# Attention scores in three PSUM tiles by turns, and one softmax shift per unit fetched by way of DRAM

## The chip, the cores and the metric

The kernel runs on one core of a Trainium2 chip. The metric is device time in microseconds (us): the median of repeated runs. A profile comes from one further execution, with its own time and span.

## What is computed

The reference is one pre-norm layer, on x of shape (2, 2048, 512) in float32: attention with 16 query heads and 2 key groups of width 32 and rotary positions, then a projection with weights and inputs rounded to fp8 e4m3. Cut to what matters:

```python
# attention: h = layernorm(x), per batch of 2048 rows
q = (h @ wq + bq).reshape(b, s, 16, 32)
k = (h @ wk + bk).reshape(b, s, 2, 32)
v = (h @ wv + bv).reshape(b, s, 2, 32)
q, k = rotary(q) * 32**-0.5, rotary(k)
scores = einsum('bqhd,bkhd->bhqk', q, repeat(k, 8)) * 32**-0.5
out = einsum('bhqk,bkhd->bqhd', softmax(scores), repeat(v, 8))
x = x + out.reshape(b, s, 512) @ wo + bo
# second half: e4m3 with one scale for all rows, one for the weight
x = x + scaled_mm(e4m3(layernorm(x)), e4m3(weight).T).astype(bfloat16)
```

A softmax does not change when a constant is taken from all scores of a query, so a kernel is free to choose the constant (the shift) as long as the exponentials neither overflow nor vanish.

## The kernel before

The work has three stages. First keys, values and the first queries are projected for one batch. Then attention runs. Then the second half rounds, transposes and multiplies all rows.

**Units.** Attention is cut into 64 units. A unit is 256 queries of four heads (a quad). It goes through 16 chunks of 128 keys, in four rounds of four chunks. One chunk is a PSUM tile of 128 keys x 4 heads x 256 queries, 1024 columns, two banks. TensorE (PE) fills it with two products of 512 columns (`probabilities`, L1022); ScalarE (ACT) takes the exponential of the tile in one instruction (L1031); VectorE (DVE) adds the two exponentials of a pair (`add_pair`, L1005). GpSimd (POOL) issues one accumulating DMA a round that adds the first pair of the round to the second (`accumulate`, L1035), and DVE joins two rounds' results (`join`, L1038). So the sums over keys are mostly made outside PE; what is left of them is summed over partitions by products with ones (`sum_up`, L986). The products of exponentials with values (`columns`, L968, 16 products a round) run one round behind (`weigh(*behind)`).

**Scores by difference.** There are two score tiles, `E` and `O`, of two banks each, taken by turns over the chunks. A tile is not cleared between chunks: the key operand `dkS` holds the difference between a key and the key 256 positions (`BACK`) earlier, so that a product added onto the tile of two chunks ago gives the scores of this chunk. Keys and queries are split into a high and a low half and stacked on the 128 rows.

**The shift.** It goes into the tile at the start of a unit, by products: `first_scores` (L523) multiplies the queries of the next unit with the first 128 keys, queries on the partitions, in rounds 0 and 1 (four products and one DVE reduction L531 each). `split_maxima` (L504, L505) splits each query's maximum for each head into two parts, `gather_maxima` transposes them on PE (L543) and copies them out of PSUM (`mT`, L547), and `probabilities` starts the first two chunks of a unit with four products each against the selector `sel` (L1013). So each query and head has a shift of its own.

**PSUM.** Eight banks: two score tiles (four), `s0` for first scores and transposes, `s1` for everything that is projected meanwhile, and two `av` banks. An `av` bank holds a unit's values in its first half and its sums in the second; units alternate between the two.

**Order.** All engines work in program order; the order is written out by hand (`tc.manual_schedule`, L1058 to L1121). In each round: chunks 0 and 1; their addition; the value products of the round before; in some rounds a sum of the unit before and its copies out of PSUM (`keep_values` L1056, the first step of `finish_heads` L939); up to two waiting VectorE pieces (`fill(ON_DVE, 2)`); chunks 2 and 3; their addition; the accumulation; the first scores in rounds 0 and 1; one or two waiting PE pieces (projection of later queries and keys, output projection, all L295) and again up to two VectorE pieces. Queries of a later quad are fetched from DRAM in round 1 (`landing`, four DMAs on SP's queue, L349). In attention, ACT issues no DMAs.

**After attention** `transposed` and `multiplied` (L1166, L1176) go through 32 tiles of 128 rows. At the end the largest sum (`seen`) is compared with a bound of 1e18 (`MOST_BITS`); only above it a second, slow path under `tc.If` computes everything again with a shift from all keys. Worked out from the reference's inputs, the sums stay far below the bound with either kind of shift.

Of the kernel before, what the change touches and what calls it, by code (L numbers as in the profile page):

```python
# [16 lines left out]
P = 128  # L17
# [10 lines left out]
def preln_attn_fp8_ffn_kernel(  # L28
# [56 lines left out]
    BACK = HB  # L85
    AV_BANKS = 2
# [24 lines left out]
    def bank(name, dtype=F32):  # L111
# [5 lines left out]
        if name[:2] in ("pk", "pq"):  # L117
            pool, tag = (ps_av, "av") if name[1] == "k" else (ps_s, "s1")
            return pool.tile(shape, dtype, tag=tag, name=name, bufs=AV_BANKS if tag == "av" else 1)
        spread[0] += 1  # L120
        return ps_t.tile(shape, dtype, tag="EO"[spread[0] % 2], name=name)
# [63 lines left out]
    sel = const.tile([P, 4, P], F32R, tag="sel", name="sel")  # L185
    nc.gpsimd.memset(sel.bitcast(F32), 0.0)
    for j in range(4):
        nc.gpsimd.memset(sel[j * HD : j * HD + 2, j, :].bitcast(F32), -1.0)
    mrow = const.tile([P, HB], F32R, tag="mrow", name="mrow")
    nc.gpsimd.memset(mrow.bitcast(F32), 0.0)  # L190
# [20 lines left out]
    def quantized_scale(amax, scale, inv, name):  # L211
# [8 lines left out]
        nc.tensor.matmul(down[:, :1], sel[:1, 0, :].bitcast(F32), whole, start=True, stop=True)  # L220
        nc.vector.tensor_scalar(scale, down[:, :1], -1.0 / E4M3_MAX, 1e-12, ALU.mult, ALU.max)
# [275 lines left out]
    split = []  # L497
    largest = {}

    def split_maxima():  # L500

        if split:
            mview, mx = split.pop()
            nc.vector.tensor_copy(mview[:, :, :, 0], mx)  # L504
            nc.vector.tensor_tensor(  # L505
                mview[:, :, :, 1], mx, mview[:, :, :, 0].bitcast(F32), ALU.subtract
            )
# [4 lines left out]


    def first_scores(u, i):

        k, half = units[u]
        if i == 0:
            largest[u] = small.tile([P, HT, 4], F32, tag="mx", name=f"mx_{u}")
        mx = largest[u]
        s = ps_s.tile([P, 4, FIRST], F32, tag="s0", name=f"s_{u}_{i}")  # L520
        at = (half * HT + i) * P
        for j in range(4):
            nc.tensor.matmul(  # L523
                s[:, j, :],
                qst[k][:, j, at : at + P],
                stacked["dkS"][:, group(k), :FIRST],
                start=True,
                stop=True,
                skip_group_check=True,
            )  # L530
        nc.vector.tensor_reduce(mx[:, i, :], s, AX.X, ALU.max)  # L531
        if i == HT - 1:
            mview = mrow.rearrange("p (i j r) -> p i j r", i=HT, j=4)
            split.append((mview, largest.pop(u)))

    maxima = {}

    def gather_maxima(u):

        split_maxima()  # L540
        tp = ps_s.tile([P, TB], F32, tag="s0", name=f"mtp_{u}")
        for i in range(HT):
            nc.tensor.transpose(  # L543
                tp[:, i * P : (i + 1) * P], mrow[:, i * P : (i + 1) * P].bitcast(F32), ident
            )
        mT = wide.tile([P, HB], F32R, tag="mT", name=f"mT_{u}")
        nc.scalar.copy(mT, tp[:, :HB])  # L547
        maxima[u] = mT
# [153 lines left out]
    with tc.manual_schedule():  # L702
# [25 lines left out]
        for i in range(HT):  # L728
            first_scores(0, i)
        run(first(kv[3], MIDDLE))  # L730
        gather_maxima(0)
        run(kv[3])

# [74 lines left out]
    seen = const.tile([P, len(units)], F32, tag="seen", name="seen")  # L808
# [125 lines left out]
    def finish_heads(u, both, sums):  # L934
# [4 lines left out]
        nc.scalar.activation(total, sums, AF.Copy, accum_out=seen[:, u : u + 1])  # L939
# [3 lines left out]
        nc.scalar.activation(guess, guess, AF.Exp, scale=-1.0)  # L943
# [63 lines left out]

    def probabilities(u, T, kc):

        k, half = units[u]  # L1010
        if kc < 2:
            for j in range(4):
# [45 lines left out]
    with tc.manual_schedule():  # L1058
        behind = None
        before = None  # L1060
        for u, (k, half) in enumerate(units):
# [13 lines left out]
            for r in range(ROUNDS):  # L1075
# [25 lines left out]
                if r == 2:  # L1101
                    split_maxima()
# [368 lines left out]
```

## Time and profile before

| | us |
|---|---|
| median of 3 runs (lowest, highest) | 1733.91 (1731.88, 1735.4) |
| the profiled execution | 1724.88 |
| its span, first to last instruction | 1723.0 |
| PE / DVE / ACT / POOL busy | 1575.1 / 1248.8 / 1236.4 / 317.1 |
| exponentials L1031, 1024 of them | 992.6 busy, 1024 ns each |
| value products L968 | 495.1 busy |
| score products L1022 | 680.0 busy, 442 ns each |
| additions L1005, 511 of them | 624.7 busy, 1223 ns each |
| granted TensorE clock from 100 to 1600 us | 1.00 |

A row of a page or an answer names line, engine and operation, what is written and read with partitions and elements, the count, then busy time and mean of one, and after the second bar the idle time before it with what ended it. TensorE's products overlap: one of them takes longer from its start to its end than the next one waits to start, so a group's cost is the distance from its start to the next group's start, not the sum of its durations. PEld is the loading of weights, which runs beside products. An arrow like `T L1022 <- ACT p L1031` reads: the products of L1022 waited for the exponential of L1031.

### The profile page before, as it was taken

How to read it: one execution, taken by the hardware profiler on the slowest of the kernel's cores; microseconds unless marked ns; L12 is line 12 of the kernel's file. 1: busy time of each engine (PE TensorE's matmuls, PEld its weight loads, DVE VectorE, ACT ScalarE, POOL GpSimd, SP SyncE). 2: the span in 40 equal slices, each digit the busy share in tenths (PEclk: the TensorE clock that was granted, in tenths of full speed). 3: DMA queues.
4: the chain of work that ended last, by engine and by line, in shares of the span. 5: the costliest groups of instructions: out<-in, count | busy, mean ns of one | idle time of the engine just before them, and what ended most of it. 6: DMA issues, size and time to landing. Idle time of an engine off the chain costs nothing.

```text
span 1723.0 us, 33241 instructions
## 1 busy us (share of the span) xinstructions
PE 1575.1 (91%) x13483; PEld 900.6 (52%) x13483; DVE 1248.8 (72%) x1673; ACT 1236.4 (72%) x1629; POOL 317.1 (18%) x381
## 2 busy tenths in 40 slices
PE   5499999999999999999999999999999989999565
PEld 2255555555555555555555555555555555555222
DVE  4447677677887769776877687767777686676697
ACT  2257877777777777777777777877777777777375
POOL 3321112211212112211221122111211122111100
PEclk9699999999999999999999999999999999999888
DMA  6657769867778767878786688656867597576222
GB/s 203 201 122 178 170 146 216 195 127 160 184 178 164 183 153 160 192 147 195 175 196 134 118 199 177 152 117 154 184 149 154 105 203 145 116 187 138 56 86 112
DMA packets 105810, 272.61 MB, mean 158 GB/s; under 512 B 15920, under 2 KB 16560, under 8 KB 102960
## 3 DMA queue, kind: packets, MB, share of 16 engines
q0 software_dynamic: 41328, 142.10, 44.2%
q1 hardware_dynamic: 61904, 126.92, 25.3%
q8 instruction: 108, 1.77, 0.4%
q10 hardware_dynamic: 2416, 1.38, 0.3%
q14 instruction: 54, 0.44, 0.1%
HBM read 87.36 MB, written 40.89 MB: 74 GB/s over the span
## 4 chain that ended last, share of the span: by engine, by line
PE 67%; DVE 10%; DMA 8%; issue 7%; ACT 5%; SPq 2%; POOL 1%; ACTq 0%; DVEq 0%; POOLq 0%
PE avs L968 23%; PE T L1022 23%; PE po L295 5%; ACT p L1031 5%; PE pq L295 4%; PE T L1013 3%; PE avs L986 3%; PE s L523 2%; DMA pa<-pa 2%; DMA qst<-q_far 2%; PE pk L295 2%; PE mtp L543 1%; DVE v L236 1%; DVE pa L1005 1%; DMA sw_q<-q 1%
## 5 line engine op out<-in xcount | busy, mean ns | idle before, releaser
L1031 ACT ACTIVATE p<-T 128x1024 f32<-128x1024 f32 x1024 | 992.6, 1024 | 178.3 <-PE T L1022 171.1
L1005 DVE TENSOR_TENSOR pa<-p,p 128x1024 f32<-128x1024 f32 x511 | 624.7, 1223 | 356.1 <-ACT p L1031 355.0
L1022 PE MATMUL T<-qst,dkS 128*128 128x512 f32 x2048 | 680.0, 442 | 24.8 <-ACT p L1031 23.8
L968 PE MATMUL avs<-p,vX 128*32 128x256 f32 x8192 | 495.1, 382 | 0.0
L1022 PEld LDWEIGHTS T<-qst,dkS 128*128 128x128 f32 x2048 | 338.7, 188 | 273.6 <-ACT p L1031 153.5
L1035 POOL DMA_DIRECT2D pa<-pa x255 | 221.0, 867 | 1201.2 <-DVE pa L1005 915.3
L968 PEld LDWEIGHTS avs<-p,vX 128*32 128x32 f32 x8192 | 239.9, 109 | 225.8 <-issue 93.9
L1038 DVE TENSOR_TENSOR pa<-pa,pa 128x1024 f32<-128x1024 f32 x125 | 152.3, 1219 | 16.0 <-DMA pa<-pa 15.9
L295 PE MATMUL po<-wo_sb,attn 128*128 128x512 f32 x256 | 129.6, 603 | 0.0
L295 PE MATMUL pq<-xnT_q,wq_sb 128*128 128x512 f32 x224 | 111.8, 601 | 0.0
L1013 PE MATMUL T<-mT,sel 128*128 128x256 f32 x512 | 94.5, 307 | 6.5 <-ACT p L1031 6.1
L1013 PEld LDWEIGHTS T<-mT,sel 128*128 128x128 f32 x512 | 72.9, 188 | 46.9 <-ACT p L1031 30.8
L986 PE MATMUL avs<-pa,ones 128*32 128x256 f32 x1048 | 80.7, 382 | 11.9 <-DVE pa L1038 11.1
L531 DVE TENSOR_REDUCE mx<-s 128x4 f32<-128x512 f32 x128 | 87.5, 683 | 2.8 <-PE s L523 2.8
L1056 ACT COPY both<-avs 128x256 f32<-128x256 f32 x64 | 23.9, 373 | 86.7 <-PE avs L986 86.7
L523 PEld LDWEIGHTS s<-dkS,qst 128*128 128x128 f32 x512 | 77.2, 192 | 14.7 <-DVE mx L531 3.1
L939 ACT ACTIVATE both<-avs 128x256 f32<-128x256 f32 x64 | 24.6, 385 | 71.7 <-PE avs L986 71.7
L523 PE MATMUL s<-dkS,qst 128*128 128x128 f32 x512 | 72.8, 265 | 2.2 <-DVE mx L531 2.1
L295 PEld LDWEIGHTS po<-wo_sb,attn 128*128 128x128 f32 x256 | 44.3, 190 | 17.6 <-issue 11.0
L986 PEld LDWEIGHTS avs<-pa,ones 128*32 128x32 f32 x1048 | 27.8, 109 | 43.7 <-DVE pa L1038 30.4
L295 PEld LDWEIGHTS pq<-xnT_q,wq_sb 128*128 128x128 f32 x224 | 39.4, 190 | 17.4 <-issue 13.5
L1171 PE MATMUL xtp<-ident_bf,xq 128*128 128x128 bf16 x128 | 16.0, 266 | 34.3 <-DVE xq L237 34.3
(128 smaller groups left out, 1033.0 us busy)
## 6 DMA issues: line engine op xcount, KB each, us to landing
pa<-pa POOLq DMA_DIRECT2D x255, 512.0 KB, 5.2
qst<-q_far SPq DMA_DIRECT2D x128, 256.0 KB, 7.0
q_far<-hi_q SPq DMA_DIRECT2D x32, 256.0 KB, 4.6
q_far<-lo_q SPq DMA_DIRECT2D x32, 256.0 KB, 4.5
x_res<-in_L_attn_x_dram SPq DMA_DIRECT2D x16, 512.0 KB, 10.8
x_res<-in_L_attn_bo_dram POOLq DMA_DIRECT2D x32, 256.0 KB, 6.7
out_dram<-v SPq DMA_DIRECT2D x16, 512.0 KB, 2.8
sw_q<-q SPq DMA_DIRECT2D x240, 32.0 KB, 3.1
```

The costliest lines, as they stand in the source:

```text
L295: nc.tensor.matmul(dst, lhs(c), rhs(c), start=(c == 0), stop=(c == chunks - 1))
L523: nc.tensor.matmul(s[:, j, :], qst[k][:, j, at : at + P], stacked["dkS"][:, group(k), :FIRST], start=True, stop=True, skip_group_check=True,)
L531: nc.vector.tensor_reduce(mx[:, i, :], s, AX.X, ALU.max)
L939: nc.scalar.activation(total, sums, AF.Copy, accum_out=seen[:, u : u + 1])
L968: nc.tensor.matmul(av[j * HD : (j + 1) * HD, :], vX[batch(k)][:, kc, group(k), :], p[:, j, :], start=(kc == 0), stop=(kc == NTS - 1), tile ...
L986: nc.tensor.matmul(dst[j * HD : (j + 1) * HD, :], ones, part[:, j, :], start=start and i == 0, stop=stop and i == len(parts) - 1, tile_pos ...
L1005: nc.vector.tensor_tensor(pa, a, b, ALU.add)
L1013: nc.tensor.matmul(T[:, j, :], sel[:, j, :], maxima[u], start=(j % 2 == 0), stop=True, skip_group_check=True,)
L1022: nc.tensor.matmul(T[:, j : j + 2, :], stacked["dkS"][:, group(k), kc * P : (kc + 1) * P], qst[k][:, j : j + 2, half * HB : (half + 1) * H ...
L1031: nc.scalar.activation(p, T, AF.Exp, scale=SCALE)
L1035: nc.gpsimd.dma_start(out=to, in_=of, accum_op=ALU.add)
L1038: nc.vector.tensor_tensor(to, to, of, ALU.add)
```

## The change

Scores go through three tiles `T0`, `T1`, `T2` by turns, so the key difference reaches back 384 positions. The first scores of a unit take a turn of their own: after 16 chunks comes a 17th turn, in which the first 128 keys meet the queries of the unit after next, keys on the partitions as in any chunk. VectorE reduces this tile to one number a partition. ACT's queue then sends the 128 numbers to DRAM (round 1 of the next unit) and fetches all of them back onto every partition (round 2); VectorE takes their maximum, scales it, and all 16 exponentials of the unit get this one number as a bias operand. The shift products, their selector, the splitting, transposes and copy of maxima are gone. There is one `av` bank instead of two, a tile that all units share: values are copied out in round 0, and the sums of a unit are formed in rounds 1 and 2 of the next (in rounds 0 and 2 before). The join of round 1 stands ahead of chunks 2 and 3 and their addition, not behind. Fetched queries are asked for in round 0. The reciprocals of the sums are accumulated into `seen` beside the sums. After attention, transposes alternate between `s1` and `av`, and products go through three tiles.

```diff
-    BACK = HB
-    AV_BANKS = 2
+    RING = 3
+    BACK = RING * P
-    def first_scores(u, i):
+    def first_scores(u, tag):
...
-        s = ps_s.tile([P, 4, FIRST], F32, tag="s0", name=f"s_{u}_{i}")
-        at = (half * HT + i) * P
-        for j in range(4):
+        s = ps_t.tile([FIRST, 4, HB], F32, tag=tag, name=f"s_{u}")
+        for j in range(0, 4, 2):
             nc.tensor.matmul(
-                s[:, j, :],
-                qst[k][:, j, at : at + P],
+                s[:, j : j + 2, :],
                 stacked["dkS"][:, group(k), :FIRST],
+                qst[k][:, j : j + 2, half * HB : (half + 1) * HB],
                 start=True,
                 stop=True,
             )
-        nc.vector.tensor_reduce(mx[:, i, :], s, AX.X, ALU.max)
+        largest[u] = small.tile([P, 1], F32, tag="mx", name=f"mx_{u}")
+        nc.vector.tensor_reduce(largest[u], s.rearrange("p j t -> p (j t)"), AX.X, ALU.max)
+    def put_largest(u):
+        far = dram.tile([P, 1], F32, tag=f"largest_{u % 2}", name=f"largest_{u}")
+        nc.scalar.dma_start(far, largest.pop(u))
+        largest_far[u] = far
+    def fetch_largest(u):
+        every = wide.tile([P, P], F32, tag="every", name=f"every_{u}", bufs=2)
+        nc.scalar.dma_start(
+            every, largest_far.pop(u).rearrange("p e -> (p e)").partition_broadcast(P)
+        )
+        shift[u] = every
+    def make_shift(u):
+        every = shift[u]
+        shift[u] = small.tile([P, 1], F32, tag="shift_u", name=f"shift_{u}")
+        nc.vector.tensor_reduce(shift[u], every, AX.X, ALU.max)
+        nc.vector.tensor_scalar(shift[u], shift[u], -SCALE, None, ALU.mult)
...
-        nc.scalar.activation(guess, guess, AF.Exp, scale=-1.0)
+        nc.scalar.activation(guess, guess, AF.Exp, scale=-1.0, accum_out=seen[:, 1, u : u + 1])
...
+    def turn_of(u, i):
+        return f"T{(u * (NTS + 1) + i) % RING}"
-        if kc < 2:
-            for j in range(4):
-                nc.tensor.matmul(
-                    T[:, j, :],
-                    sel[:, j, :],
-                    maxima[u],
...
+        if kc < RING:
+            scores[kc] = ps_t.tile(
+                [P, 4, HB], F32, tag=turn_of(u, kc), name=f"T_{u}_{kc}"
+            )
+        T = scores[kc % RING]
...
-                start=False,
+                start=kc < RING,
...
-        nc.scalar.activation(p, T, AF.Exp, scale=SCALE)
+        nc.scalar.activation(p, T, AF.Exp, bias=shift[u], scale=SCALE)
...
+    avs = ps_av.tile([P, 2, HB], F32, tag="av", name="avs")
...
-                while r == 1 and landing:
+                while landing:
                     landing.pop()()
...
-                probs = [probabilities(u, banks[0], chunks[0])]
-                probs.append(probabilities(u, banks[1], chunks[1]))
+                probs = [probabilities(u, kc) for kc in chunks[:2]]
+                if r == 1 and 1 < u + 1 < len(units):
+                    put_largest(u + 1)
+                if r == 2 and 1 < u + 1 < len(units):
+                    fetch_largest(u + 1)
                 pair = add_pair(u, chunks[0], *probs)
                 if behind:
                     weigh(*behind)
                 if before and r == 0:
-                    parts = before.far[1 : 2 if in_two(before.u) else 3]
-                    sum_up(before.avs[:, 1, :], parts, False, False)
                     keep_values(before)
+                elif before and r == 1 and in_two(before.u):
+                    sum_up(avs[:, 1, :], before.far[1:2], False, False)
                 elif before and r == (2 if in_two(before.u) else 1):
-                    sum_up(before.avs[:, 1, :], before.far[3:], False, True)
...
+                    sum_up(avs[:, 1, :], before.far[3 if in_two(before.u) else 1 :], False, True)
+                    finishing.append(Job(finish_heads(before.u, before.both, avs[:, 1, :])))
                 fill(ON_DVE, 2)
-                if r == 2:
-                    split_maxima()
                 if last:
                     join(unit.far[1], unit.far[0])
+                elif before and r == 1 and in_two(before.u):
+                    join(before.far[3], before.far[2])
+                if last:
                     if u + 1 < len(units):
-                        gather_maxima(u + 1)
-
-                probs.append(probabilities(u, banks[0], chunks[2]))
-                probs.append(probabilities(u, banks[1], chunks[3]))
+                        make_shift(u + 1)
+
+                probs += [probabilities(u, kc) for kc in chunks[2:]]
                 if not (last and whole):
                     unit.far.append(add_pair(u, chunks[2], *probs[2:]))
                     accumulate(unit.far[r], pair)
                 add_some_bias()
-                if before and r == 1 and in_two(before.u):
-                    join(before.far[3], before.far[2])
                 behind = unit, chunks, probs
-                if r < HT and u + 1 < len(units):
-                    first_scores(u + 1, r)
+                if last and u + 2 < len(units):
+                    first_scores(u + 2, turn_of(u, NTS))
```

## The prediction

> **What bounds the kernel now.** The page's busy times come first, then the score line's own view, which says when attention begins and ends.
>
> ```profile
> PE 1575.1 (91%) x13483; PEld 900.6 (52%) x13483; DVE 1248.8 (72%) x1673; ACT 1236.4 (72%) x1629; POOL 317.1 (18%) x381
> ```
>
> ```profile
> L1031 ACT ACTIVATE p<-T x1024: 1003/1024/1062, 100.0 to 1605.3; 128x1024 f32<-128x1024 f32 x171
> ...
>   PE T L1022: 171.1, 316
> ...
>   PEld T L1022: 153.5, 372
>   PEld T L1013: 30.8, 62
> ```
>
> The exponentials run from 100.0 to 1605.3 + 1.0 us: 64 units in 1506.3 us, **23.5 us a unit**. Ahead lie 100 us, behind 116.7. PE looks full (91%), yet its products wait for ACT (the last two lines) and ACT's exponentials wait for PE (171.1): the two engines take turns. A unit's turns show in TensorE's timeline (start, length, then the group):
>
> ```profile
> 806.92 1.93 PE L968 MATMUL avs<-p,vX 128*32 128x256 f32 x32
> 808.79 0.44 PE L543 MATMUL mtp<-ident,mrow 128*128 128x128 f32 x2
> 808.98 1.18 PE L1022 MATMUL T<-qst,dkS 128*128 128x512 f32 x4
> 810.00 1.88 PE L295 MATMUL po<-wo_sb,attn 128*128 128x512 f32 x4
> 811.32 1.04 PE L1013 MATMUL T<-mT,sel 128*128 128x256 f32 x4
> 812.19 0.63 PE L1022 MATMUL T<-qst,dkS 128*128 128x512 f32 x2
> 812.66 0.64 PE L1013 MATMUL T<-mT,sel 128*128 128x256 f32 x4
> 813.14 0.63 PE L1022 MATMUL T<-qst,dkS 128*128 128x512 f32 x2
> 813.70 1.93 PE L968 MATMUL avs<-p,vX 128*32 128x256 f32 x32
> 815.45 0.61 PE L986 MATMUL avs<-pa,ones 128*32 128x256 f32 x8
> 815.99 1.20 PE L1022 MATMUL T<-qst,dkS 128*128 128x512 f32 x4
> 817.03 0.56 PE L523 MATMUL s<-dkS,qst 128*128 128x128 f32 x4
> 817.42 1.07 PE L295 MATMUL po<-wo_sb,attn 128*128 128x512 f32 x2
> ```
>
> Start to start is what a group costs when nothing is waited for. A chunk's two score products: 812.19 to 812.66, 0.47. A round's value products: 1.87 and 1.75, say 1.81. A sum: 0.54. One projection step: (1.88 - 0.59) / 3 = 0.43. So a unit's PE work is 16 x 0.47 = 7.5, plus 4 x 1.81 = 7.2, plus two sums 1.1, plus 480 projection steps over 64 units (7.5 x 0.43 = 3.2), plus the shift's products and the first scores 1.9 (next part), plus some 0.3 for the later keys: **21.2 us. The other 2.3 of the 23.5 are stalls.** The waits view allows this: products and loads wait 214 us for L1031 in all (153.5 + 30.8, and 29.9 on PE itself), 3.3 a unit, part of it under running products, and the sums wait 41.5 us for the joins (L1038).
>
> **The change, part by part (us per unit).**
>
> *Products removed.* The shift by product (L1013): 812.66 to 813.14, 0.48 a tile, two tiles: 0.96. Its transposes (L543): 0.19. The first scores (L523): 817.03 to 817.42, 0.39, twice: 0.78. Added: the 17th turn, two products like L1022: 0.47. PE net **-1.46**, 93 us over 64 units, all on the engine that is busiest. PE work becomes 19.8.
>
> *Three score tiles.* With two, chunk c+2 may not begin before the exponential of c ends: first product 0.24, its tail 0.40, exponential 1.02, and a wake of about 0.1: 1.75 from start to start. In a round's first half the value products cover that; in its second half PE has only 0.94 of scores and 0 to 0.9 of projection, and the second exponential ends 0.9 later still. Hence the 2.3 of stalls. With three, the chunk waits for an exponential one turn older (0.9 to 1.0 earlier), which covers nearly all of it. I leave 0.2 of score waits; bounds: 0, and the 2.3 of now.
>
> *Bias by pointer.* The exponentials take the shift as a per-partition bias. No row has an exponential with one; the nearest are a copy without and an ACTIVATE with, both 512 wide out of PSUM:
>
> ```profile
> L439 ACT ACTIVATE q<-pq,bq_sb 128x512 f32<-128x512 f32 x32 | 22.1, 689 | 3.7 <-PE pq L295 3.7
> ...
> L285 ACT COPY xnT_kv<-tp_kv 128x512 f32<-128x512 f32 x32 | 18.9, 590 | 20.8 <-PE tp_kv L282 20.8
> ```
>
> 0.10 each, so 1024 to about 1120 ns, and 16 x 0.10 = +1.6 on ACT. ACT's own sum: 16 exponentials 0.92 apart now (two in 1.94), 1.02 then: 16.3; keeping the values 0.37, the sums 0.39 + 0.19, Ln and Exp 0.84, a second accumulator read 0.19, query and key work 0.8; the mT copy (0.37) goes: 19.1. The two DMA issues: 0.5 to 0.7 each on ACT's queue in the prologue's rows, so between 0 (issued while an exponential runs) and 1.2; I take 0.3, since each stands behind an exponential of 1.1. ACT 19.4: just under PE. The added cost is hidden by PE only as long as PE is the slower; were ACT never hidden, 1.6 + 0.3 less 0.2 would be 1.7 a unit, 109 us.
>
> *The trip through DRAM.* The put stands behind exponential 5, the fetch behind 9, the shift's reduce in round 3, its use a round later. Behind the fetch on ACT wait the sums' copy and exponentials 10 and on; for them PE. The put has about a round, 5.2, to land. Rows for small transfers:
>
> ```profile
> sw_q<-q SPq DMA_DIRECT2D x240, 32.0 KB, 3.1
> ...
> bkv_sb<-in_L_attn_bk_dram ACTq DMA_DIRECT2D x1, 0.2 KB, 7.1
> ...
> bq_sb<-in_L_attn_bq_dram ACTq DMA_DIRECT2D x1, 2.0 KB, 11.1
> ```
>
> The last two ran at the start beside whole-block loads. I take the first, nearest in time and load: no wait. Bounds 0 and 11.1 - 5.2 = 5.9. The Trainium skill ("DMA: Bandwidth & Descriptors", "Anatomy of one DMA") puts the fixed cost of a DMA at about 2 us whatever its size; by it the sum has no wait at all, by the 11.1 row it has 5.9 a unit, and only the run can tell. The same page (Specifications) speaks against the put: runs under 512 B are read, modified and written, and this one writes 4-byte runs. Before unit 0 the trip costs a put and a fetch of 3 each around the key projection that fills 89.9 to 96.5 now: +0.5 in all.
>
> *VectorE.* Off: two reduces of 0.68 and two small operations of 0.17. On: one reduce of twice the width (about 1.28), one of 128 wide (under 0.3), one tiny multiply: even. DVE stays at 17.3 (1106 us busy from 100 to 1600, 63.8 units). But the new reduce stands behind the addition of chunks 14 and 15, and chunk 2 of the next unit needs its tile. After exponential 15 ends: addition 1.2, reduce 1.3, then PE may go on; PE gets there after two chunks' scores and the values, some 2.2 after the same moment, and round 3 on DVE (two additions, join, shift, reduce, fillers: over 6 us in a 5.2 us round) comes late. I price this **new stall at 0.7**, bounds 0 and 2 (a late filler piece of 1.2 more).
>
> *Joins and sums.* Two sums stay, one moved from round 0 to 1; the round 1 join stands ahead of an addition, so the sum of round 2 finds it done: of the 0.65 a unit of join waits 0.2 stays. In return the join comes about 5 us after its accumulation was issued, not 7.8 to 9.8 as now (six units from 350 to 480 us); landing takes 4.5 to 12.4, median 5.2. DVE will wait 0.5 to 1 there; its spare 3 us a unit hide it, else 1.0 x 64 = 64 us. One bank: values are copied out a round before the next values begin, so nothing waits. Query loads go to SP a round earlier and wait there for the old tile; what stands behind them on SP is needed later: 0. The epilogue's tiles: within 2 us.
>
> **The sum.** PE 19.8, stalls 0.2 + 0.7 + 0.2, and 0.2 for DMA slots and uneven units: **21.1 us a unit**, 1350 us. Span 1723.0 - 1506.3 + 1350 + 0.5 = 1567; with the 1.9 around it 1569. The profiled execution (1724.9) was 9 us quicker than the median of the runs (1733.9): 1578, say **1580**.
>
> **Rivals.**
> *Waits change place.* Only the products come off; the stall moves to ACT (longer exponentials) or the unit's border. 23.5 - 1.46 = 22.0 a unit: 1408, so 1637; with half of ACT's 1.7 showing, 1690. For it: ACT 19.4 against 19.8 is a tie, DVE with its DMA waits 18.5. Against: a third tile breaks just this turn-taking.
> *All stalls go.* 19.8 a unit: 1267, 1495. Against: the border stall.
> *The transfers hold the pace.* The windows view has the DMA engines 75% busy from 100 to 1600, 17.7 us a unit; at 21.1 that is 84%. If accumulations land so late that DVE stands, little is gained: 1690 to 1735.
> *Slower: the fetch blocks ACT.* If the put lands in 11.1, ACT has 19.4 + 5.9 = 25.3 a unit, 1.8 x 64 = 115 over now: 1850. It decides from a landing of about 5.2 + 4.1 = 9.3, where ACT reaches 23.5. Against: 32 KB moves in 3.1 under the same load.
>
> **Chances.** Forecast (1535 to 1610) 0.60; waits change place (1610 to 1690) 0.20; all stalls go (below 1535) 0.08; transfers 0.05, of which 0.03 within 0.2%; slower 0.07. Faster 0.90, same 0.03, slower 0.07 (0.2% is about what a measurement can tell from no change). Range: the forecast's own (0.60), the second up to 1670 (0.16) and the third down to 1525 (0.04): 1525 to 1670.
>
> **What would show it.** Right: PE's score products wait for L1031 under 60 us in all; exponentials near 1120 ns; a unit near 21; PE waiting for the first-score reduce about 0.7 a unit. Wrong: ACT idle behind its own DMA issue (put landing over 5), ACT busy without gaps at over 20 a unit, joins waiting for accumulations by more than 1.5 a unit, or score waits that stay.

## The result and the profile after

| | before | after |
|---|---|---|
| median of 4 runs (lowest, highest) | 1732.89 (1729.06, 1735.4) | 1866.03 (1854.8, 1875.69) |
| the profiled execution, its span | 1724.9, 1723.0 | 1865.6, 1863.8 |
| one unit, mean | 23.5 | 25.6 |
| granted TensorE clock, 300 to 1400 us | 1.00 | 0.93 |

The change makes the kernel slower: ratio 1.077, 95% interval 1.070 to 1.083. The forecast was 1580 with a range up to 1670. Busy times of the kernel after:

```profile
PE 1540.3 (83%) x12459; PEld 844.5 (45%) x12459; DVE 1249.2 (67%) x1609; ACT 1290.2 (69%) x1629; POOL 316.0 (17%) x376
```

Every engine now has more idle time than before. The exponentials' own view (minimum, median, maximum in ns; below, who waited for them):

```profile
L1025 ACT ACTIVATE p<-T,shift x1024: 1093/1114/1179, 106.7 to 1744.9; 128x1024 f32<-128x1024 f32 x171
...
  PEld T L1016: 129.6, 154
  PE T L1016: 64.9, 78
```

They have become as long as predicted (1114 ns at the median; 1115 on average). The new idle time lies elsewhere. From the DMA issues of the kernel after (KB each, median us from issue to landing):

```profile
largest<-mx ACTq DMA_DIRECT2D x64, 0.5 KB, 9.6
```

The prediction gave the put "about a round, 5.2, to land"; by this row it takes 9.6. The view tells the landing of only 11 of the 64 puts. A put adds 16 counts to its semaphore as it lands, and by these counts 59 puts can be timed: their median is 8.8, the shortest 7.0. ScalarE's timeline shows what that does to one unit:

```profile
789.77 0.33 ACTq L520 DMA_DIRECT2D largest<-mx  x1
790.47 1.12 ACT L1025 ACTIVATE p<-T,shift 128x1024 f32<-128x1024 f32 x1
792.72 4.13 ACT L1025 ACTIVATE p<-T,shift 128x1024 f32<-128x1024 f32 x4 [1.13 <-PE T L1016]
800.24 0.33 ACTq L526 DMA_DIRECT2D every<-largest  x1
801.74 0.39 ACT L930 ACTIVATE both<-avs 128x256 f32<-128x256 f32 x1 [4.89 <-PE avs L977]
```

The put goes out at 789.77. The last exponential ahead of the fetch ends at 796.85, but the fetch is not issued before 800.24: the put landed at 800.22. For 58 of the 59 puts that can be timed the fetch starts within 0.1 us of the landing. The chain of waits over the same stretch (start, length, what) shows that the put is not alone:

```profile
785.66 14.07 DMA pa<-pa
799.73 0.02 issue
799.76 1.24 DVE pa L1032
```

An accumulation issued 4 us ahead of the put took 14.07 us and landed within half a microsecond of it; the join waited for it, and the sum products for the join. The windows view of the stretch (length, busy us of PE, PEld, DVE, ACT and POOL with instruction counts, granted clock, DMA share, GB/s):

```profile
796.80:801.00 4.20, 0.00 (x0) 0.00 (x0) 1.24 (x2) 0.05 (x1) 0.00 (x0) 1.00 1.19 47
801.00:803.00 2.00, 1.97 (x12) 1.31 (x13) 2.00 (x2) 1.26 (x4) 0.59 (x2) 0.78 0.43 55
803.00:806.20 3.20, 3.20 (x6) 1.39 (x5) 2.07 (x3) 1.73 (x2) 1.17 (x2) 0.61 1.08 144
```

For 4.2 us TensorE does nothing, while the DMA engines count as fully busy and move 47 GB/s. They are busy with packets of other transfers that take longer than usual. The accumulations go in 32,640 packets of 4096 bytes, of which the median takes 0.33 us; here 764 of them take over 1 us, 730 of these while a put is on its way, against 8 in the kernel before. In this unit the put's own packets take 0.02 us at most. TensorE's timeline, to set beside the one of before:

```profile
794.80 1.93 PE L959 MATMUL avs<-p,vX 128*32 128x256 f32 x32
801.03 0.64 PE L977 MATMUL avs<-pa,ones 128*32 128x256 f32 x8 [4.30 <-DVE pa L1032]
801.60 1.67 PE L1016 MATMUL T<-qst,dkS 128*128 128x512 f32 x4
803.07 3.10 PE L291 MATMUL pq<-xnT_q,wq_sb 128*128 128x512 f32 x4
```

After the stop it goes on at a clock of 0.78 and 0.61: four projection steps take 3.10, where before the change four took 1.88. TensorE has 36 stops of over 2.5 us between 120 and 1600, where the kernel before has none; the granted clock averages 0.64 in the 5 us behind them and 1.00 in the 5 us ahead of them. In units 4 to 58 the mean time from exponential 9 to 10, where the fetch stands, went from 2.9 to 5.0 us.

### The profile page after: what moved, and what is told of

Same layout as the page of the kernel before. It is cut to its first block, busy times and chain, and to the rows that moved or that the text cites. A ratio compares the mean times of both kernels' runs of the same rounds, so it can differ in the third digit from the quotient of the medians.

```text
span 1863.8 us, 31217 instructions
## 1 busy us (share of the span) xinstructions
PE 1540.3 (83%) x12459; PEld 844.5 (45%) x12459; DVE 1249.2 (67%) x1609; ACT 1290.2 (69%) x1629; POOL 316.0 (17%) x376
## 4 chain that ended last, share of the span: by engine, by line
DMA 29%; PE 18%; DVE 17%; issue 16%; ACT 9%; SPq 5%; POOL 3%; ACTq 0%; DVEq 0%; POOLq 0%
DMA pa<-pa 10%; DMA largest<-mx 9%; PE T L1016 7%; ACT p L1025 7%; PE avs L959 5%; DMA sw_q<-q 4%; SPq L304 4%; DVE pa L996 4%; DVE pa L1032 2%; PE po L291 2%; POOL pa L1029 2%; DMA qst<-q_far 2%; PE pq L291 2%; DVE mx L515 1%; PE avs L977 1%
## 5 line engine op out<-in xcount | busy, mean ns | idle before, releaser
L1025 ACT ACTIVATE p<-T,shift 128x1024 f32<-128x1024 f32 x1024 | 1070.0, 1115 | 197.4 <-PE T L1016 137.3
L1016 PE MATMUL T<-qst,dkS 128*128 128x512 f32 x2048 | 726.0, 473 | 118.2 <-ACT p L1025 64.9
L1016 PEld LDWEIGHTS T<-qst,dkS 128*128 128x128 f32 x2048 | 375.3, 199 | 429.7 <-issue 176.4
L959 PE MATMUL avs<-p,vX 128*32 128x256 f32 x8192 | 511.2, 391 | 0.0
L930 ACT ACTIVATE both<-avs 128x256 f32<-128x256 f32 x63 | 24.2, 384 | 200.5 <-PE avs L977 99.9
L515 DVE TENSOR_REDUCE mx<-s 128x1 f32<-128x1024 f32 x64 | 77.9, 1218 | 2.6 <-PE s L507 2.6
L309 DVE SCALAR_TENSOR_TENSOR sw_q<-sw_q,sign,cs 128x512 f32<-128x512 f32 x30 | 22.5, 750 | 71.6 <-DMA sw_q<-q 49.8
L291 PEld LDWEIGHTS pq<-xnT_q,wq_sb 128*128 128x128 f32 x224 | 45.9, 205 | 23.5 <-issue 15.1
L507 PE MATMUL s<-qst,dkS 128*128 128x512 f32 x128 | 41.7, 409 | 5.5 <-DMA qst<-q_far 4.8
L278 PE MATMUL tp_kv<-ident,xn_kv 128*128 128x128 f32 x128 | 23.1, 325 | 27.4 <-DVE xn_kv L259 27.2
L291 PE MATMUL pk<-xnT_kv,wkv_sb 128*128 128x512 f32 x64 | 39.6, 738 | 7.3 <-ACT xnT_kv L281 7.3
L1177 PE MATMUL py<-wT,xqT 128*128 128x512 bf16 x128 | 43.1, 471 | 0.3 <-ACT xqT L1169 0.3
```

Source lines behind the costliest of these rows:

```text
L291: nc.tensor.matmul(dst, lhs(c), rhs(c), start=(c == 0), stop=(c == chunks - 1))
L507: nc.tensor.matmul(s[:, j : j + 2, :], stacked["dkS"][:, group(k), :FIRST], qst[k][:, j : j + 2, half * HB : (half + 1) * HB], start=True, ...
L515: nc.vector.tensor_reduce(largest[u], s.rearrange("p j t -> p (j t)"), AX.X, ALU.max)
L959: nc.tensor.matmul(av[j * HD : (j + 1) * HD, :], vX[batch(k)][:, kc, group(k), :], p[:, j, :], start=(kc == 0), stop=(kc == NTS - 1), tile ...
L1016: nc.tensor.matmul(T[:, j : j + 2, :], stacked["dkS"][:, group(k), kc * P : (kc + 1) * P], qst[k][:, j : j + 2, half * HB : (half + 1) * H ...
L1025: nc.scalar.activation(p, T, AF.Exp, bias=shift[u], scale=SCALE)
```

## The experiments

Ratios are to the kernel before, measured beside each run.

| run | us | ratio, 95% interval |
|---|---|---|
| e1_no_trip | 1680.9 | 0.971 (0.969 to 0.973) |
| e2_put_early | 1853.7 | 1.073 (1.070 to 1.075) |
| e3_trip_on_sp | 1816.4 | 1.050 (1.046 to 1.053) |
| e4_join_back | 1854.2 | 1.073 (1.071 to 1.075) |
| e7_put_act_fetch_sp | 1880.6 | 1.090 (1.086 to 1.095) |
| e8_rows_apart | 1684.6 | 0.976 (0.973 to 0.980) |
| e9_whole_rows | 1681.4 | 0.973 (0.969 to 0.977) |
| e11_scores_ahead_no_trip | 1673.4 | 0.969 (0.966 to 0.973) |
| e5_pointer_before | 1756.5 | 1.015 (1.012 to 1.018) |
| e6_two_tiles_no_trip | 1879.2 | 1.087 (1.084 to 1.090) |
| e12_repair | 1705.0 | 0.986 (0.983 to 0.989) |
| e13_repair_old_join | 1742.2 | 1.009 (1.006 to 1.012) |
| e15_rows_scores_ahead | 1679.4 | 0.971 (0.968 to 0.973) |
| e16_no_accumulation | 1599.0 | 0.925 (0.922 to 0.927) |
| e17_turn_later | 1653.6 | 0.957 (0.954 to 0.959) |
| e18_join_later | 1695.1 | 0.981 (0.978 to 0.984) |
| e19_join_and_turn_later | 1644.5 | 0.952 (0.950 to 0.954) |
| e20_four_runs | 1650.9 | 0.956 (0.954 to 0.957) |

### What the trip costs

**e1**: the shift is made of a tile of zeros; no put, no fetch; first scores and their reduction stay.

```diff
-        every = shift[u]
+        every = still
...
-                    put_largest(u + 1)
...
-                    fetch_largest(u + 1)
```

> The changed kernel without the trip through DRAM: no put, no fetch; VectorE makes the shift from a constant tile of zeros with the same two instructions, so the shift is 0 in every unit (first scores and their reduce still run, their result is not used). Theory A (the fetch holds ACT's queue until the put has landed, 9.6 us against a round of some 5; the other waits of the changed kernel, for joins, sums and the clock, follow from that stop): the interval behind exponential 9 falls from 5.0 to about 2.3 us, a unit from 25.6 to 22.3, the time to about 1655 (1620 to 1700). Rival B (the accumulations land later, joins and sums wait for them; the trip itself is beside the point): joins still wait 90 us and the time stays above 1780. Rival C (the longer exponentials and the 17th turn cost more than the products that went): 1733 or more even without the trip.

Measured: 1680.9, that is 185 us under the changed kernel, 2.9 a unit. From exponential 9 to 10 it takes 2.3 us. The trip is what makes the change slower. Without it the change gains 3%, not the 9% forecast; the second part of this section is about that.

**e2**: put a round earlier, behind the copy of the values.

```diff
-                if r == 1 and 1 < u + 1 < len(units):
-                    put_largest(u + 1)
...
                 if before and r == 0:
                     keep_values(before)
+                    if 1 < u + 1 < len(units):
+                        put_largest(u + 1)
```

> The trip stays on ACT's queue, but the put is issued in round 0, behind the copy of the values, instead of round 1; the fetch stays in round 2, so the put has two rounds, about 10.5 us, to land against 7.4 to 12.4 measured. Theory A: most of the stop goes, within 40 us of the kernel without the trip: 1655 to 1710. Rival B: no gain, 1840 to 1880. Rival C: above 1733.

Measured: 1853.7. The median landing of the 59 puts that can be timed is 9.8, and for 47 of them the fetch still starts within 0.1 us of it; from exponential 9 to 10 it takes 4.4 us. Theory A fell short: more time ahead was eaten by the same slow put.

**e3**: both transfers on SyncE's queue (`nc.sync` for `nc.scalar`, twice).

> Put and fetch are issued on SP's queue in the same rounds instead of ACT's. Theory A: ACT no longer stops; SP stops some 4 us a unit instead, which its loads feel only here and there: 1660 to 1760. Rival B: no gain, 1840 to 1880. Rival C: above 1733.

Measured: 1816.4. The put takes 10.9 there. ScalarE's stop shrinks to 2.9 us, but the shift comes late: exponentials wait 139 us for it, and the step over the border (from exponential 15 to the next unit's first) takes 3.9 us, against 2.5 without a trip. The stop moved with the queue.

**e4**: the join of round 1 back behind the addition.

> Only the round 1 join goes back behind the addition of chunks 2 and 3, where the kernel before had it; all else as changed. Theory A: the sums' 210 us of waiting for the joins are a consequence of the stop, so little changes: 1840 to 1885. Rival B (the join ahead of the addition makes VectorE wait for accumulations, 92 us now, and so the sums): joins stop waiting and 60 to 120 us come back, 1750 to 1805.

Measured: 1854.2, some 12 us under the changed kernel; the stop of 5.0 us stays. The join is not the cause.

**e7**: e2's put, and the fetch on SyncE in round 2, so that nothing on ScalarE stands behind a fetch.

```diff
-        nc.scalar.dma_start(
+        nc.sync.dma_start(
             every, largest_far.pop(u).rearrange("p e -> (p e)").partition_broadcast(P)
```

> The put goes out on ScalarE's queue in round 0 behind the copy of the values (as in e2), the fetch on SyncE's queue in round 2. Theory A (the whole price of the trip is a queue of work held by a fetch that waits for a put of about 10 us; the bytes cost nothing): nothing waits on ScalarE now, the put has 11 to 12 us before its fetch is reached, the fetch lands 5 us later and ahead of the shift, and the stop behind exponential 9 of a unit (5.0 us in the changed kernel, 2.3 without a trip) goes; 1681 to 1710 us, the kernel without the trip being 1681. Rival B (a trip costs in any queue, because SyncE's own transfers are held as ScalarE's exponentials were): 1760 to 1820 us, the interval behind exponential 15 above 3 us as with both transfers on SyncE (3.9 us, 1816 us).

Measured: 1880.6, so both theories missed the time, A by far: with nothing waiting for the put on ScalarE the kernel is no faster. B's sign came, 3.0 us behind exponential 15. SyncE's queue, now the one that stands, waits 565 us in all for puts at the fetch. From the engines' waits (engine and line waiting, released by; us in total, times, longest):

```profile
ACT both L930 <- PE avs L977: 150.3, 52, 7.9
DVE pa L1032 <- DMA pa<-pa: 135.6, 46, 8.1
```

VectorE now waits 135.6 us for accumulations (53.3 without a trip), and the sum products and ScalarE wait behind it. In the trace it is the accumulations beside the put that land late: that of round 3, just ahead of a put in round 0, lands after 8.7 on average and that of round 0 after 8.5; without a trip 6.6 and 6.3. In the changed kernel, with the put in round 1, it is that of round 0: 9.3. Of the accumulations' packets 413 take over 1 us in e7, 9 without a trip. A fetch that blocks is thus only one road; the put itself holds other transfers. What each of the two costs in time, no run tells apart.

**e8 and e9**: is it the put's 4-byte runs, the place that they go to, or the queue? e8 writes the same 128 runs of 4 bytes 512 bytes apart, e9 whole rows of 512 bytes; both fetch only the first row.

```diff
-        nc.scalar.dma_start(far, largest.pop(u))
+        nc.scalar.dma_start(largest_far[u % 2][:, :1], largest.pop(u))   # e8, far is 128 x 128
+        nc.scalar.dma_start(far, largest.pop(u))                         # e9, both 128 x 128
```

> The put writes its 128 values of 4 bytes 512 bytes apart, into the first column of a 128 x 128 tensor in DRAM, and not into 512 bytes in a row; the fetch reads the first row of that tensor, so that the shift is made of the maximum of one key and of zeros, not of all keys. Queue, place and number of packets are those of the changed kernel. Theory A1 (the put takes 9.6 us because 128 writes of 4 bytes into the same 512 bytes follow one another): landing 2.5 to 4.5 us, no stop behind exponential 9, 1685 to 1730 us. Theory A2 (a write of 4 bytes is slow wherever it goes): landing 8 to 11 us, 1845 to 1875 us.

> The put writes 128 whole rows of 512 bytes (64 KB: the maximum in the first column, zeros in the others) from 128 partitions; the fetch reads the first of them, so that the shift is made of the maximum of one key and zeros. Theories A1 and A2 (one 512-byte stretch, or 4-byte writes): landing 3 to 5.5 us, as other writes to DRAM of this kernel have it (3 to 5.7 us), and 1690 to 1740 us. Theory A3 (ScalarE's queue lands late whatever it carries): landing stays at 8 to 11 us, 1845 to 1880 us.

Measured: 1684.6 and 1681.4, both the time without a trip. The put's row in e8 and, after it, in e9:

```profile
largest<-mx ACTq DMA_DIRECT2D x64, 0.5 KB, 3.5
```

```profile
largest<-rows ACTq DMA_DIRECT2D x64, 64.0 KB, 3.8
```

Same queue, same place, same number of packets in e8: only the distance between the 4-byte runs differs, and the landing falls from a median of 8.8 (9.6 in the row) to 3.5. In e9 the accumulations are back at 6.6, 5.7, 6.0 and 6.7 on average by round. The accumulations' packets of over 1 us are 14 in e8 and 10 in e9, not 764. **A1 holds**: 128 writes of 4 bytes into one 512-byte stretch are slow together; small writes alone are not. How far apart they have to lie, no run shows. The prologue agrees: the first put of the changed kernel went out at 92.0 with the DMA engines at a share of 0.04, and still took 7.4; those of e8 and e9 there took 1.4 to 1.6. That put's last packet had started 1.0 us after the issue, but its 16 counts came from 4.1 to 7.4 us (1.3 to 1.4 in e8): the time is spent after the packets are sent.

**e20** brings all 128 maxima through, with e17's edits (below): VectorE turns them into four rows, and the put is four runs of 128 bytes.

```diff
+        nc.vector.transpose(largest[u], mx)          # 128 x 32, by blocks of 32 x 32
...
-        far = dram.tile([P, 1], F32, ...)
-        nc.scalar.dma_start(far, largest.pop(u))
+        far = dram.tile([4, 32], F32, ...)
+        nc.scalar.dma_start(far, largest.pop(u)[::32, :])
```

> e17 with all 128 maxima brought through, as the change does it: VectorE turns the column of maxima by 32 x 32 blocks into four rows of 32, and the put writes four runs of 128 bytes into the one 512-byte stretch; the fetch reads the 512 bytes. Theory A1 (it is the number of writes into one stretch that takes the put's time): 4 in place of 128, landing 3 to 5 us, VectorE 0.1 to 0.3 us more per unit, 1645 to 1670 us: a version that computes what the changed kernel computes and beats the kernel before by 3.5 to 5%. Rival (any writes of parts of one stretch follow one another with the same price whatever their number, or the transposition on VectorE at the border costs): landing 7 to 10 us and above 1750 us, or 1670 to 1700 us.

Measured: 1650.9, ratio 0.956. The transposition takes 0.21 us a unit. The put adds five counts to its semaphore here, and the last comes 3.4 us after the issue at the median, 1.6 in the prologue. The fetch starts 5.3 us behind the put at the median, as in e17. Four writes into one stretch are harmless where 128 are not; whether their number decides or their length, the run does not tell. This version computes what the changed kernel computes and beats both.

### Why 3% and not 9%

**e11**: e1 with the first scores and their reduction ahead of the addition of chunks 14 and 15; **e15**: e9 with the same edit.

```diff
+                if last and u + 2 < len(units):
+                    first_scores(u + 2, turn_of(u, NTS))
                 if not (last and whole):
                     unit.far.append(add_pair(u, chunks[2], *probs[2:]))
```

> The kernel without the trip (shift from zeros, no put, no fetch; 1681 us), and the 17th turn with its reduction stands ahead of the addition of chunks 14 and 15 in VectorE's order. Theory A (the border stall of 1.8 us per unit, 68.1 us of weight loads and 44.9 us of products waiting for the reduction, is the reduction held behind an addition that waits for the last exponential): these waits fall below 25 us together, the interval behind exponential 15 falls from 2.5 to about 1.5 us, and the time is 1570 to 1620 us. Rival B (the reduction's own length, or TensorE and its clock, sets the border; the stall moves on to the exponentials): 1650 to 1681 us.

> e9 (the put of whole rows, in its place of round 1) with the first scores and their reduction ahead of the addition of chunks 14 and 15: the two edits that helped, together. From e9's 1681 us and the 7 us by which e11 is under the kernel without a trip: 1665 to 1682 us, faster than the kernel before by 2.5 to 4%. This is also the base of the three runs that follow.

Measured: 1673.4 and 1679.4. The waits for the reduction in e1:

```profile
PEld T L1015 <- DVE mx L517: 68.1, 52, 5.3
PE T L1015 <- DVE mx L517: 44.9, 18, 4.8
```

In e11 these 113 us fell to 51, but the time by only 7 us, and in e15, against e9, by 2. Theory A fell: a wait that is long on one engine's list was mostly not what ended last.

**e5** and **e6** price two parts alone: a pointer bias in the kernel before, and two score tiles in e1.

```diff
-        nc.scalar.activation(p, T, AF.Exp, scale=SCALE)
+        nc.scalar.activation(p, T, AF.Exp, bias=none, scale=SCALE)   # e5
...
-    RING = 3
+    RING = 2                                                          # e6
```

> The kernel before the change, with a column of zeros given as the bias of each of its 1024 exponentials of chunks, and nothing else: the price of the pointer operand alone, where two score tiles take turns. The exponentials go from 1024 to about 1115 to 1120 ns. Theory A (ScalarE has slack, the 0.1 us lie beside the products): 1727 to 1750 us. Rival B (with two tiles the products of a chunk wait for the exponential two chunks before, and each 0.1 us is paid): 1.6 us per unit, 1815 to 1840 us.

> The kernel without the trip (1681 us) with two score tiles by turns and not three. Theory A (the third tile is what takes the score waits away, 2.3 us per unit in the kernel before, and what of the change is a gain comes from there): 1750 to 1830 us, with ScalarE's waits for scores and the weight loads' waits for exponentials at 2 us per unit or more. Rival B (the third tile is worth little, because the work between the turns of a pair is longer than an exponential): 1681 to 1715 us.

Measured: e5 1756.5, 25 us over the kernel before, 0.4 a unit, between the theories: a quarter of the 1.6 shows. e6 1879.2, 198 us over e1, above what theory A allowed: 286 us of weight loads wait for exponentials, against 82 in e1. So the third tile is worth 3.1 a unit in this order of work, which has 17 turns and longer exponentials.

**e12** put, fetch and shift each a round earlier, on e15; **e13** has the old join too.

```diff
-                if last:
+                if r == 2:
                     if u + 1 < len(units):
                         make_shift(u + 1)
```

> The put of whole rows (as in e9, so that the shift is made of one key's maximum and zeros), issued in round 0 and fetched in round 1, the shift made in round 2 and not in round 3, and the first scores with their reduction ahead of the addition of chunks 14 and 15. Theory A (what is left above the products' own time, 1.5 us of 22.9 per unit, is ScalarE and TensorE waiting for what VectorE delivers late at the border: 51 us for the shift, 113 us for the reduction): both waits go and the time is 1600 to 1640 us. Rival B (VectorE's own lateness, held by transfers that it waits for, 53 us behind the accumulations and 24 us behind the swapped queries, shows in the next thing that is needed from it, the tiles of probabilities or the sum products): 1650 to 1675 us.

> e12 with the join of round 1 back behind the addition of the round's last two chunks, where it was before the change. Theory B of e12 (VectorE held by the moved join, which waits 53 us for accumulations and in the kernel before only 16): VectorE's wait for accumulations falls from 53 to about 15 us and the time is 20 to 50 us under that of e12. Rival (the join's place is worth what it was in e4, 12 us, or less): within 15 us of e12.

Measured: 1705.0 and 1742.2. In e12 the step over the border falls from 2.5 to 1.7 us, but the steps in rounds 0 and 1 grow by more (behind exponential 1 from 1.9 to 2.5, behind 5 from 2.3 to 2.8), and the fetch, now a round behind its put, blocks ScalarE again seven times (34.6 us). e13 is a miss: with the old join the sum products wait 154 us for it, and the time rises by 37. In this order the join's new place is better than the old; in e4, beside the slow put, the old one was 12 us better.

More is seen when units are sorted by VectorE's work in e9 (mean length of a unit in us, from its first exponential to that of the next; the same units in every kernel):

| VectorE busy in the unit | units | before | e9 | e17 | e16 |
|---|---|---|---|---|---|
| under 16 | 26 | 23.1 | 21.5 | 21.7 | 21.1 |
| 16 to 19 | 21 | 23.8 | 23.4 | 22.1 | 21.5 |
| over 19 | 17 | 23.8 | 24.4 | 23.5 | 22.4 |

Units with little on VectorE gained 1.6; those with much of it, where queries are turned or a block is finished, lost 0.6. The longest of the second kind and one of the first in the windows view of e9 (columns as above):

```profile
842.90:871.50 28.60, 20.39 (x153) 11.69 (x154) 22.05 (x28) 19.66 (x25) 8.36 (x11) 0.88 0.93 214
1116.40:1137.20 20.80, 20.68 (x186) 11.78 (x186) 15.35 (x17) 18.18 (x23) 3.45 (x4) 1.00 0.81 159
```

The lower one runs TensorE without a gap; in the upper one VectorE has 22.05 us to do, and TensorE idles for 8.

**e16** leaves the accumulations out, so that its sums lack half of their terms; **e17** lets the rotation of swapped queries and keys come three rounds after their transfer, not two; **e18** puts the second join and its sum product a round later; **e19** is e17 and e18.

```diff
-        nc.gpsimd.dma_start(out=to, in_=of, accum_op=ALU.add)                     # e16
...
-                beside.insert(0, Job(turn(n, m, raw, u, csb), due=step[0] + 2))
+                beside.insert(0, Job(turn(n, m, raw, u, csb), due=step[0] + 3))   # e17
...
-                elif before and r == 1 and in_two(before.u):
+                elif before and r == 2 and in_two(before.u):                      # e18
                     join(before.far[3], before.far[2])
```

> e15 without its 255 accumulating transfers of 512 KB: the additions of chunk pairs stay, but of each round's two only one reaches the sum, so that the denominators lack half. Theory A (the 1.5 us per unit that TensorE still idles come from transfers that land late: VectorE waits 53 us for accumulations and 24 us for swapped queries, and holds TensorE and ScalarE meanwhile): VectorE's waits for transfers fall from about 80 us below 15 us and the time is 1580 to 1625 us. Rival B (it is the amount and order of VectorE's own work, up to 22 us of a 23.5 us unit where a block is finished or queries are turned): 1645 to 1680 us.

> e15 with the rotation of swapped queries and keys due three rounds after their transfer was asked for, not two. Theory A (part of it: VectorE's 24 us for swapped queries, each wait of up to 4 us at a border where the shift and the reduction stand behind it): the wait falls below 8 us and the time is 15 to 35 us under e15. Rival B: within 8 us of e15.

> e15 with the second join of a unit in round 2 and its second sum product in round 3, one round later each. Theory A (the other part: VectorE's 53 us for accumulations, in the join that the change put a few us earlier): the wait falls below 15 us and the time is 15 to 45 us under e15. Rival B (VectorE's wait ends nothing last): within 8 us of e15, or above it where the sum products now crowd round 3.

> e17 and e18 in one: the rotation due three rounds after its transfer, the second join and its sum product a round later. In e18 VectorE's wait for accumulations fell from 74 to 22 us, but that for swapped queries rose from 24 to 48 us. Theory A (VectorE's late transfers are what is left, and each has to be given time): both waits together fall below 30 us, and the time goes under e17's 1654 us, to 1615 to 1645 us. Rival B (the later join crowds the border whatever the queries do): 1655 to 1690 us.

Measured: e16 1599.0 and e17 1653.6, 26 under e15, both as their theory A has it; in e17 VectorE's 24.2 us for swapped queries are gone altogether. e18 1695.1, 16 over e15, so its theory A fell: the wait for accumulations became short, but another grew. Accumulations and swapped queries in the waits of e15 and, after them, of e18:

```profile
DVE pa L1035 <- DMA pa<-pa: 73.7, 40, 6.2
DVE sw_q L309 <- DMA sw_q<-q: 24.2, 15, 4.6
```

```profile
DVE pa L1035 <- DMA pa<-pa: 21.6, 12, 4.7
DVE sw_q L309 <- DMA sw_q<-q: 48.5, 13, 9.2
```

e19 1644.5: with both given time, one short wait remains of the two kinds (21.9 for accumulations), and it is the fastest kernel here that leaves no part of the sums out (its shift, as in all runs built on e9, is made of one key's maximum). Theory A holds, at the slow end of its numbers. So late transfers explain 35 of the 99 us that e15 lies above the forecast, through VectorE, which works in order. How much of e16's 80 us are waits, and how much is that GpSimd and the DMA engines have less to do (share 0.33, not 0.80, from 300 to 1400), stays open.

## Why the prediction was wrong

**The trip** is the step that failed. It was costed at no wait, from the row of the swapped queries (3.1 for 32 KB) as "nearest in time and load". Measured: a landing of 8.8 at the median, and 185 us, 2.9 a unit. The nearest rows by *layout* were the two set aside, single values to a partition, with 7.1 and 11.1; and the direction and place of the write were not in any row. The rival "the fetch blocks ACT" gave 1850 for a landing of 11.1, and 1866 came. That its number is so near is luck: by its own sum a landing of 8.8 gives ACT 19.4 + 3.6 = 23.0 a unit, less than the 23.5 of the kernel before. What that sum leaves out is that the put holds other transfers, the accumulations above all, and that TensorE's clock is lower after a stop. Its chance of 0.07 was much too small all the same, since nothing but one row spoke against it.

The Trainium skill ("DMA: Bandwidth & Descriptors", "Specifications") has writes under 512 bytes read, modified and written. That spoke against this put, but by itself it would condemn e8 too, whose 4-byte writes land in 3.5; what was slow is many of them in one 512-byte stretch. The fixed cost of about 2 us that the prediction names, which the page gives for transfers issued by GpSimd, is near what the spread writes took on idle engines (1.4 to 1.6) and far from this put's 7.4. The same page ("Queues, rings and completion order") says that the count of a finished transfer lands only after every earlier write of that DMA engine. The accumulations that land together with the put fit that; no run here isolates it, and their packets, too, take longer.

**A slack that was a mean.** This is a second step that failed, and alone it would have left the range: e1, without the trip, takes 1680.9. DVE's waits for accumulations were priced, but "its spare 3 us a unit hide it". Their size was right: 0.8 a unit without the trip (53.3 / 64; priced 0.5 to 1). But VectorE has 15 us of work in some units and over 20 in others, and there much less is left to hide behind. The change also made more depend on VectorE at the border: the shift and the reduction that frees a score tile now stand in its queue. That this is the reason is shown in part: giving two kinds of late transfers time (e19) brings 35 us, and the rest stays open. The forecast's 21.1 was built from one unit's groups and nearly holds for the light ones (21.5); the mean without the trip is 22.9. That is 1.8 x 64 = 115 us. With the trip's 185 it makes 300, against a miss of 286. The forecast had also added 11 us because the profiled execution before ran 9 us under the median; in e1 its median and its profiled execution lie within 1.5 us.

**The other steps.** Exponentials: 1120 predicted, 1115 measured. Their cost, taken as hidden, with 1.7 a unit if not: 0.4 in e5. VectorE even: 1248.8 and 1249.2 busy. The third tile: 2.1 a unit taken, 3.1 in e6. The border stall: 0.7 taken, 1.8 in e1's waits, of which e11 and e15 give back 0.1 at most. Score waits: 0.2 taken; in e1 loads and products still wait 82.2 and 25.0 us for exponentials, 1.7 a unit if added up as the prediction added them (3.3 before), part of it under running products. The trip ahead of unit 0: 0.5 us taken, about 6 measured (the first exponential starts at 106.7, in e1 at 100.5). The join: better in its new place than in the old without the slow put (e13), a round later better still once the queries have time (e19 against e17, 9 us), and wrong as free. The products removed were not tried alone.

## What to carry to other kernels

Price a new transfer by the row that is nearest in layout (bytes per run, how many runs to one place in memory), not in size or time, and where no row has it, let the blocked queue weigh as much as the free one. Here a column of single values went out well once it was turned into four rows. A slack counts only in the stage where the wait falls: sort the units by the load of the engine that is to hide it. A long wait on a list is not yet time; only moving it shows whether something else ends at the same moment.

## What the runs showed of the hardware

128 writes of 4 bytes to consecutive addresses in DRAM took 7.4 us with idle DMA engines and 8.8 at the median in attention; 512 bytes apart they took 1.4 and 3.5, and four writes of 128 bytes into one stretch 1.6 and 3.4. The accumulations issued just ahead of the late puts (round 0) landed after 9.3 us on average, not 6.3 as in e1, and 764 of the accumulations' packets took over 1 us, not 9. In one such stretch the DMA engines count as busy at 47 GB/s. And a stop of TensorE costs twice: behind 36 stops of over 2.5 us the granted clock averaged 0.64 over the next 5 us; over the run the same number of products took 1540.3 us busy after and 1481.7 in e1, at mean granted clocks of 0.923 and 0.959.
